# Selective scan in a vision stack: projection copies moved to the ends of units five and six, the copy of y behind the exps, the second projection behind the last spread

## The chip, the cores and the metric

The kernel runs on one core of a Trainium2 chip. The metric is device time in microseconds for one execution, given as the median of several. The engines are named as the profile names them: PE (TensorE matmuls), PEld (its weight loads), DVE (VectorE), ACT (ScalarE), POOL (GpSimd) and SP (SyncE, which here issues nearly all DMAs).

## The reference, cut to what matters

Four layers work on an image batch of shape (8, 64, 64, 96). Each layer normalises over channel groups, computes a residual and adds it. Layers 0 and 2 are selective scans in four directions: over rows, over columns, and both backwards. Layer 1 is a chunked scan, layer 3 a spectral filter with an expansion to 384 channels. The changed code belongs to the selective scan, whose core is this recurrence over the 4096 positions, for each direction k, each of 192 channels d and 16 states n:

```python
def step(h, inp):
    ut, dt, bt, ct = inp
    dA = jnp.exp(dt[..., None] * A4)
    dBu = (dt * ut)[..., None] * bt[:, :, None, :]
    h = h * dA + dBu
    y = jnp.einsum('bkdn,bkn->bkd', h, ct)
    return (h, y)
```

Here `dt` is a softplus of a projection of u, and `bt` and `ct` are two further projections of u. The sum of y over the four directions is kept.

## The kernel before, in words

The batch is a Python loop over eight images. For each image `selective_scan` is called twice (layers 0 and 2), so there are 16 passes. From the second image on, the last layer of the image before is laid in small operations (the class `Beside`) among the steps of the scan: 14 of the 16 passes have such work beside them.

A pass has 32 steps, one for each chunk: four directions k times eight chunks of 512 positions. In directions 1 and 3 the chunk is read along the columns of the image, so that its access to u and y is strided (`wh` is true). A chunk is made of six units: 32 channels times 16 states each, as 128 partitions times four groups of 512 positions. The loop `for t in range(total + 2)` goes over the units; n is the unit within the chunk (0 to 5), i the chunk. "The fifth and sixth unit" of the title are n = 4 and n = 5.

The order on every engine is the order in which the code emits the instructions (`tc.manual_schedule()`); an engine's queue works strictly in that order and waits by semaphores. Nothing is reordered by a planner.

What one unit needs:

- `spread` (L834): a matmul that lays 32 channels of delta times u over 128 partitions, into the PSUM tile pu. It shares a single buffer, tag "misc", with some operations of `Beside`.
- `with_b` (L840): the product of that with b, into db. Two units of three do it on DVE from pu, the third on POOL from a copy du2.
- `decays` (L855): two exps on ACT for each half of a unit, into the PSUM tile da of that half. There are only two such tiles, so the exps of a half can't begin before the scan of the same half of the unit before has ended.
- `scan` (L870): the recurrence on DVE, in two halves (p = 0 and 1); each half waits for its da and for db.
- `leave` (L886, L891): ACT copies the last state, POOL multiplies h by c in place.
- `total_y` (L898, L908): after three units PE sums over the states into the PSUM tile py; ACT then copies it to y (L993 for the first three units, L1007 for the others).

The PSUM tile py has the tag "py" and a single buffer. The same buffer serves the two projections pv of a coming chunk and some operations of `Beside`.

`prepare(i)` makes a chunk's inputs in parts, as a generator that is advanced by `prepare_part`. The parts, each ending at a `yield`, are: (1) the first projection, L742, into pv; (2) its copy into raw, L747, and the second projection, L751; (3) the copy of that, L755, its store to DRAM (bcd, L757) and the four loads of b (L764); (4) softplus, L775, and the stores of dd; (5) the loads of dx for the first three units (L782) and of c; (6) delta times u on POOL (L793, L799), its store and the loads of du2; (7) the loads of dx for the last three units (L782). SP issues these DMAs in the order of the code and stops at each until what it waits for has happened.

In the step of chunk i, part 1 of chunk i + 2 is emitted at the beginning of unit 4, part 2 in the middle of unit 5 (between the exps of its first and second half), part 3 in the middle of unit 0 of the next step, after `total_y` has been emitted; parts 4 and 5 at the ends of units 0 and 1, part 6 in unit 3, part 7 at the end of unit 5.

## Time and profile before

| | |
|---|---|
| median of three runs | 27086.93 us (27085.17 to 27111.33) |
| the profiled execution's own time | 27082.74 us |
| its span | 27080.9 us |
| instructions | 283056 |
| DVE busy | 23966.2 us, 88% |
| PE busy | 22624.0 us, 84% |
| POOL busy | 21781.7 us, 80% |
| ACT busy | 16539.7 us, 61% |
| scan halves on DVE (L870) | 6144, 2282 ns each |
| DVE idle just before a scan half | 900.6 us in all |
| granted TensorE clock, mean | 0.773 of full |

Times come from one profiled execution. A row of a group of instructions reads: line, engine, operation, output and inputs, shapes, count, then busy microseconds and the mean of one in nanoseconds, then the idle time of that engine just before them and what ended it. A row of the table of waits reads: who waited, for whom, microseconds in total, how often, the longest. A row of the timeline reads: start in microseconds, duration, engine, line, operation and count; in brackets the engine's idle time before it and what ended that. A row of the table of stretches gives for each engine the busy microseconds, then the granted TensorE clock, the share of the DMA engines and GB/s. PE's busy time is modelled, since matmuls are pipelined: a busy PE is not one at its peak.

### The profile page before, as it was taken

To read this page: it belongs to the slowest core of one execution; us is meant where nothing else is said; L and a number is where in the kernel's file an instruction comes from. 1 tells how busy PE (TensorE), PEld (TensorE's weight loads), DVE (VectorE), ACT (ScalarE), POOL (GpSimd) and SP (SyncE) were. 2 spreads that over 40 slices of the span, in tenths; PEclk is the share of its full clock that TensorE was granted. 3 is DMA by queue.
4 is the path that set the end of the run, shared out by engine and by line. 5 is a ranking of instruction groups with operands and counts; after the bars stand their busy time and mean duration, and the time that the engine had idled before them with its cause. 6 is when DMAs were issued, how large, how long until landed. Compare 5 with 4: busy or idle time off the path is not lost. (4 is left out here: it accounts for less than half of the span.)

```text
span 27080.9 us, 283056 instructions
## 1 busy us (share of the span) xinstructions
PE 22624.0 (84%) x91061; PEld 8150.5 (30%) x91061; DVE 23966.2 (88%) x17105; ACT 16539.7 (61%) x29953; POOL 21781.7 (80%) x8360
## 2 busy tenths in 40 slices
PE   7787788888888888888888888888888888888888
PEld 2141122422224222242222422224222342223424
DVE  8989899798997989979898898988989889898896
ACT  5656566466665656556565565655656556565564
POOL 8949898498984979859797697976979769797694
PEclk7687777877778777787777877778777787778878
DMA  4415454154541545415453254532545325453252
GB/s 121 119 30 124 114 130 117 31 131 122 132 111 35 133 117 137 103 44 132 116 136 98 50 132 118 135 92 56 133 119 134 85 62 133 118 134 78 70 133 67
DMA packets 1681704, 2831.72 MB, mean 105 GB/s; under 512 B 434984, under 2 KB 478280, under 8 KB 1675616
## 3 DMA queue, kind: packets, MB, share of 16 engines
q1 hardware_dynamic: 1663584, 2807.32, 41.9%
q8 instruction: 730, 11.96, 0.2%
q10 hardware_dynamic: 16640, 6.29, 0.1%
q14 instruction: 750, 6.14, 0.1%
HBM read 2385.11 MB, written 427.49 MB: 104 GB/s over the span
## 5 line engine op out<-in xcount | busy, mean ns | idle before, releaser
L870 DVE TENSOR_TENSOR_SCAN h<-da,db 128x1026 f32<-128x1026 f32 x6144 | 13765.8, 2282 | 900.6 <-ACT da L855 479.2
L891 POOL TENSOR_TENSOR h<-h,c 128x2048 f32<-128x2048 f32 x3072 | 12769.4, 4174 | 726.0 <-ACT state L886 510.1
L908 PE MATMUL py<-h,cst 128*32 128x512 f32 x24576 | 5301.4, 795 | 69.9 <-POOL h L891 69.8
L855 ACT ACTIVATE da<-dx,a2s 128x512 f32<-128x512 f32 x6144 | 4236.4, 690 | 1508.7 <-DVE h L870 1366.6
L855 ACT ACTIVATE da<-dx,a0s 128x512 f32<-128x512 f32 x6144 | 4235.8, 690 | 1481.8 <-DVE h L870 1344.3
L840 POOL TENSOR_TENSOR db<-du,b 128x2048 f32<-128x2048 f32 x1024 | 4648.2, 4539 | 567.6 <-ACT db L826 567.6
L840 DVE TENSOR_TENSOR db<-pu,b 128x2048 f32<-128x2048 f32 x2048 | 4643.9, 2268 | 110.9 <-PE pu L834 100.6
L834 PE MATMUL pu<-du,cst 32*128 32x512 f32 x4096 | 3239.2, 881 | 1007.4 <-DVE db L840 799.9
L908 PEld LDWEIGHTS py<-h,cst 128*32 128x32 f32 x24576 | 1175.0, 142 | 4827.3 <-issue 4517.4
L751 PE MATMUL pv<-u,wk 96*128 96x512 f32 x2048 | 1816.9, 1030 | 688.4 <-ACT raw L747 685.8
L898 PE MATMUL py<-y,cst 96*96 96x512 f32 x1536 | 1517.0, 1084 | 397.9 <-ACT raw L755 395.4
L834 PEld LDWEIGHTS pu<-du,cst 32*128 32x128 f32 x4096 | 790.4, 239 | 3079.7 <-issue 1361.9
L742 PE MATMUL pv<-u,wk 96*96 96x512 f32 x2048 | 1452.4, 838 | 186.7 <-ACT y L993 142.6
L1285 ACT ACTIVATE sg<-sg 128x768 f32<-128x768 f32 x1024 | 819.6, 800 | 859.1 <-PE sg L1269 859.1
L993 ACT COPY y<-py 96x512 f32<-96x512 f32 x512 | 417.5, 815 | 1411.4 <-PE py L908 1411.4
L516 PE MATMUL ps<-s,w3as 96*128 96x512 f32 x1344 | 912.4, 767 | 327.7 <-ACT sf L523 188.1
L1239 POOL TENSOR_TENSOR ce<-ec,cr 112x512 f32<-112x512 f32 x256 | 530.8, 2074 | 719.1 <-ACT ec L1237 700.8
L1317 DVE TENSOR_TENSOR wt<-wt,cbm 128x768 f32<-128x768 f32 x1024 | 985.3, 997 | 136.6 <-ACT wt L1286 136.1
L886 ACT COPY state<-h 128x4 f32<-128x4 f32 x3072 | 597.5, 194 | 782.5 <-DVE h L870 776.8
L751 PEld LDWEIGHTS pv<-u,wk 96*128 96x128 f32 x2048 | 540.6, 291 | 1740.2 <-ACT raw L747 1212.5
L319 POOL TENSOR_SCALAR xn<-xs,sb 96x512 f32<-96x512 f32 x192 | 198.1, 1033 | 991.7 <-PE pz L324 495.6
L1216 POOL TENSOR_TENSOR rr<-lr,cc 128x768 f32<-128x768 f32 x256 | 376.6, 1471 | 754.1 <-ACT lr L1214 749.2
(241 smaller groups left out, 30790.9 us busy)
## 6 DMA issues: line engine op xcount, KB each, us to landing
dx<-dd SPq DMA_DIRECT2D x4096, 192.0 KB
b<-bcd SPq DMA_DIRECT2D x2048, 256.0 KB
c<-bcd SPq DMA_DIRECT2D x2048, 256.0 KB
du<-dud SPq DMA_DIRECT2D x2048, 128.0 KB
dd<-raw SPq DMA_DIRECT2D x1024, 192.0 KB
dud<-du SPq DMA_DIRECT2D x512, 128.0 KB
xd<-xs SPq DMA_DIRECT2D x256, 192.0 KB
cr<-bcd SPq DMA_DIRECT2D x1536, 32.0 KB
```

The source lines that it names most:

```text
L516: nc.tensor.matmul(ps, w3as[:, m * 128 : (m + 1) * 128], live["x2"], start=True, stop=True)
L742: nc.tensor.matmul(pv[:DM], weights[k][:, hi, 128:], uv[hi], start=(hi == 0), stop=(hi == 1))
L751: nc.tensor.matmul(pv, weights[k][:, hi, :128], uv[hi], start=(hi == 0), stop=(hi == 1))
L834: nc.tensor.matmul(pu, sel[rows, :], m["du"][rows, n // 3, :], start=True, stop=True)
L840: (nc.gpsimd if pool else nc.vector).tensor_mul(groups(m["db", n]), (m["du2"][:, n // 3, :] if pool else m["pu"]) .unsqueeze(1) .to_broadc ...
L855: nc.scalar.activation(dst[:, g, :LC], made[i]["dx"][n // 3][:, n % 3, :], AF.Exp, scale=av4[:, k, n, gs : gs + 1],)
L870: nc.vector.tensor_tensor_scan(made[i]["h", n][:, at][:, way], das[p][:, rev : 2 * SEG + rev][:, way], made[i]["db", n][:, at][:, way], 0. ...
L891: nc.gpsimd.tensor_mul(h, h, made[i]["c"])
L898: nc.tensor.matmul(py, skip[:, hf, :] if k == 0 else ident[:DM, :DM], view((u if k == 0 else y)[:, hf, :], wh, c * LC, LC), start=True, st ...
L908: nc.tensor.matmul(py[32 * q : 32 * q + 32, :], red, hs[q][:, g, :], start=False, stop=(g == NSG - 1),)
L1285: nc.scalar.activation(sg, sg, AF.Abs)
L1317: nc.vector.tensor_mul(it["wt"], it["wt"], m["cbm"][:, j : j + 1, :].to_broadcast([128, RK, Q]),)
```

## The change

`prepare` gets one more `yield`: the copy of the first projection (L747) and the second projection (L751) become parts of their own, so that there are eight parts. In the step of chunk i they are now emitted as follows, for chunk i + 2: the first projection at the beginning of unit 4, as before; its copy at the end of unit 4; the second projection at the beginning of unit 5, right after that unit's spread; its copy, the store of bcd and the loads of b at the end of unit 5, ahead of the last part of chunk i + 1 (the dx loads of its last three units). The part in the middle of unit 0 is gone. The copy of y (L993) moves from the beginning of unit 4 to behind the exps of unit 5's first half, which unit 4 emits. On PE, DVE and POOL the order of the instructions stays what it was; ACT and SP are reordered.

```diff
@@ prepare
                 raw = tp.tile([128, 2, LC], F32, name="raw")
                 nc.scalar.copy(raw[:DM, 1, :], pv[:DM])
+                yield
 
                 pv = pyp.tile([128, LC], F32, name="pv", tag="py")
@@ before the loop
-                for _ in range(5):
+                for _ in range(6):
                     prepare_part(0)
...
-                for _ in range(2):
+                for _ in range(4):
                     prepare_part(1)
@@ the loop over units
                     elif n == 4:
-                        nc.scalar.copy(*sums)
                         if quota > 3:
                             other.begin(pmp, "misc")
                         prepare_part(i + 2)
-                    if n == 5:
+                    elif n == 5:
+                        prepare_part(i + 2)
                         other.end()
                     if t < total:
                         scan(t, 0)
...
                     elif n == 4:
+                        nc.scalar.copy(*sums)
                         other.end()
-                    elif n == 0:
-                        prepare_part(i + 1)
-                    elif n == 5:
-                        prepare_part(i + 2)
                     if t < total:
                         scan(t, 1)
                         leave(t, n == 3)
...
                     if n in (1, 2):
                         other.end()
+                    if n in (4, 5):
+                        prepare_part(i + 2)
                     if n in (0, 1, 5):
                         prepare_part(i + 1)
```

## The prediction

> **What bounds the kernel now.** I read the page's busy shares first, then its costliest groups, then the table of waits, then the timeline of single steps.

> ```profile
> PE 22624.0 (84%) x91061; PEld 8150.5 (30%) x91061; DVE 23966.2 (88%) x17105; ACT 16539.7 (61%) x29953; POOL 21781.7 (80%) x8360
> ...
> L870 DVE TENSOR_TENSOR_SCAN h<-da,db 128x1026 f32<-128x1026 f32 x6144 | 13765.8, 2282 | 900.6 <-ACT da L855 479.2
> L891 POOL TENSOR_TENSOR h<-h,c 128x2048 f32<-128x2048 f32 x3072 | 12769.4, 4174 | 726.0 <-ACT state L886 510.1
> ```

> DVE leads. The 6144 scan halves make 512 steps (16 passes of 32 chunks), each of six units u0 to u5. Per step DVE has 13765.8/512 = 26.9 us of scans and 4643.9/512 = 9.1 us of spreads times b (L840), 36.0 in sum; POOL has (12769.4 + 4648.2 + 737.1 + 615.2)/512 = 36.7, some 0.2 less where its instructions overlap. From one first scan half to that of the next chunk a step lasts 37.5 to 37.7 us on average and never under 36.2. So about 1.3 us of a step are waits of DVE, and POOL is free for about 1 us: no reordering can bring more than about 1 us x 512, some 500 us. The waits sit where one scan follows another with no spread product between them: before u5 (mean 0.72 us in the two passes without the last layer's operations beside, 0.44 to 0.47 in the others) and before u2 (0.62; 0.49 to 0.54). The table of waits names their neighbours:

> ```profile
> ACT y L993 <- PE py L908: 1411.4, 477, 6.6
> PE pv L751 <- ACT raw L747: 685.8, 432, 3.3
> PE py L898 <- ACT raw L755: 551.1, 479, 3.6
> DVE h L870 <- ACT da L855: 479.2, 563, 7.8
> ```

> ACT stands at the copy of y until TensorE has summed py, with the exps of u5 behind it; TensorE stands at the second projection and at the next total of y until ACT copies raw. Two steps show it, first one whose chunk is read along the rows ("plain"), without work beside:

> ```profile
> 261.13 4.48 DVE L870 TENSOR_TENSOR_SCAN h<-da,db 128x1026 f32<-128x1026 f32 x2
> ...
> 264.30 0.58 ACT L993 COPY y<-py 96x512 f32<-96x512 f32 x1 [3.81 <-PE py L908]
> 264.78 1.41 ACT L855 ACTIVATE da<-dx,a0s 128x512 f32<-128x512 f32 x2
> ...
> 264.93 1.96 PE L742 MATMUL pv<-u,wk 96*96 96x512 f32 x4 [0.75 <-ACT y L993]
> ...
> 266.28 4.48 DVE L870 TENSOR_TENSOR_SCAN h<-da,db 128x1026 f32<-128x1026 f32 x2 [0.66 <-ACT da L855]
> ...
> 266.82 1.12 PE L834 MATMUL pu<-du,cst 32*128 32x512 f32 x2
> ...
> 270.67 2.27 DVE L840 TENSOR_TENSOR db<-pu,b 128x2048 f32<-128x2048 f32 x1
> ```

> Then one whose chunk is read along the columns ("transposed", every second run of eight chunks), with work beside:

> ```profile
> 4386.01 4.48 DVE L870 TENSOR_TENSOR_SCAN h<-da,db 128x1026 f32<-128x1026 f32 x2
> ...
> 4388.39 1.05 ACT L993 COPY y<-py 96x512 f32<-96x512 f32 x1 [3.02 <-PE py L908]
> ...
> 4389.49 3.65 PE L742 MATMUL pv<-u,wk 96*96 96x512 f32 x4 [0.17 <-ACT y L993]
> ...
> 4393.08 2.07 PE L834 MATMUL pu<-du,cst 32*128 32x512 f32 x2
> ...
> 4395.18 2.29 DVE L840 TENSOR_TENSOR db<-pu,b 128x2048 f32<-128x2048 f32 x1
> ```

> Let z be the end of u4's first scan half (263.4; 4388.3) and W the start of the product with the next chunk's first spread (270.67; 4395.18). A second chain runs beside the scans: py ready, copy of y (one PSUM buffer, py, serves both), first projection, spread, product at W. In the plain step the spread was ready at 267.94, 2.7 us early. In the transposed step it ended at 4395.15 and the product began 0.03 later: there TensorE sets W already.

> **The change part by part.** [...]Durations are of this one execution, 27,082.7 us by its own time (span 27,080.9), 4.2 below the median of 27,086.9.

> 1. Copy of y behind u5's exps. The exps need z, end at z+1.47 and release scan u5 at once: W can then be z+6.5 (lowest value seen 6.47). But the copy cannot begin before z+1.47. Over 464 inner steps py ended at z-0.3 on average, and in 429 before z+1.36: in those y now waits for the exps and the first projection starts later than it could. The new chain is fixed: z+1.47, copy 0.58 (plain) or 1.05 (transposed), 0.06 to start, projection 1.96 or 3.65, spread 1.12 fast or 2.07 slow.
>    - Plain: 2.11 + 1.96 + 1.12 = z+5.2, below 6.5, so W = z+6.5. W before: z+7.21 without work beside (29 steps, scaled from 464 to 512), 7.03 with (131). Gain 0.71 x 29 + 0.53 x 131 = 90 us.
>    - Transposed: 2.58 + 3.65 - 0.1 (overlap) + about 1.9 = z+8.1. W before: 7.45 (26 steps), 7.08 (131). Loss 0.65 x 26 + 1.02 x 131 = 151 us. The cover of the late copy, the early start of this projection, is what is taken away.
>    - Plain copy with a transposed projection (chunks six and seven of a plain run): 2.11 + 3.65 + 1.6 = z+7.3 against 7.30 (9) and 6.63 (46): loss 31.
>    - Steps in which a second operation of the last layer comes ahead of that spread (139): its matmuls, its copy and the spread add about 3.2 us after the first projection where that is transposed. z+6.9 against 6.83 (70), 9.2 against 8.94 (15), 9.4 against 8.93 (54): loss 5 + 4 + 25 = 34.
>    - Sum +126 us. Where py is late, u4's remaining ACT work (side copy, state, exps' second half) now ends later than scan u5's second half wants: about +10.

> 2. Projection copies at the ends of u4 and u5 (fifth and sixth). The first copy waits for the first projection; queued behind it on ACT are the next chunk's first exps, the state of u5 and, after that, POOL's last product with c. The exps end at most 0.62 + 1.42 after the projection; the scan that wants them comes after a spread (1.1 at least) and a product (2.27): covered by construction. POOL takes up that last product at z+8.3 (263.37 + 8.29); the state is there at about z+8.5 in the worst, transposed case: nothing, at most 0.3 us of POOL's 1 us of slack. The second copy waits for the second projection (3.78 from the spread's end) and ends 4.4 after it; the exps behind it are wanted 2.27 + 2.24 = 4.5 after it: nothing.

> 3. Second projection behind the spread with no wait for ACT: the next total of y starts 1.0 us earlier (its idle before: 1.0 to 1.24 per step). The wait before u2 falls to 0.34, which stays, since there the exps follow the softplus with its two table loads. Gain 0.28 x 64 + 0.15 x 224 + 0.20 x 224 = 96 us.

> 4. SP. The store of bcd and the four b loads now stand ahead of the four dx loads for units u3 to u5, which before were issued at about z+4.3. In a transposed step: copy done z+12.6, b issued z+14.3 to 16.1, dx to z+17.9. The stretch 1018.5 to 1024 moved 199 GB/s at a DMA share of 0.81, some 240 GB/s when full, so b (1.05 MB), dx (0.79) and dd (0.39) are through by about z+24.3. u3's exps want dx at z+24.4 and delay a scan only after z+27.4, since a product precedes it. Cost 0; bounds 0 to +1 us per step. du, c and the first dx load have over 10 us of slack.

> 5. Before each pass one more copy and b's load: 16 x 0.6 at most, beside the convolution. Nothing.

> [...] TensorE's clock comes in whole stretches:

> ```profile
> 262.90:269.70 6.80, 4.29 (x15) 0.98 (x9) 6.14 (x4) 4.42 (x9) 6.80 (x3) 1.00 0.46 129
> 269.70:283.40 13.70, 11.83 (x23) 3.02 (x26) 13.49 (x7) 10.06 (x18) 13.70 (x4) 0.50 0.42 99
> ```

> (The column before the DMA share is the granted clock.) In the row the full clock outlives py's end (264.18) by 5.5 us. [...]

> Sum: 126 + 10 + 30 - 96 = +70: 27,082.7 + 70 = 27,153, say **27,150 us**, 0.23% above the median. 0.2% (54 us) is about what a measurement of this kernel can tell from no change.

> **Rivals.**
> - As worked out, chance 0.40: 27,040 to 27,260, since the transposed spread is uncertain by half a microsecond over 157 steps and the rest by as much again. 0.22 of it slower, 0.16 within the bound, 0.02 faster.
> - Faster, 0.30: the clock holds through the transposed projection, the spread takes 1.1 and W is z+7.2 instead of 8.1. 157 x 0.9 + 55 x 0.4 = 163 us less: 26,990; with plain steps keeping the clock on into the second projection and the total of y, 26,900. It decides where the full clock lasts beyond z+7.2. For: TensorE now runs on from the projection to the total of y without a pause. Against: in the transposed step the clock fell at 4393.0 with TensorE busy throughout. 0.05 of it stays within the bound.
> [...]
> - Slower by the dx loads, 0.05: they land after z+27.4 and the scan of u3 waits, 0.5 us x 512: 27,410. Against: 3 us of room by the sum above.

> Together: faster 0.02 + 0.25 = 0.27; within 0.16 + 0.05 = 0.21; slower 0.22 + 0.25 + 0.05 = 0.52. Below 26,880 and above 27,430 I leave about 0.1 each. Range 26,880 to 27,430.

> **What would show it.** Right: no wait of DVE before u5; the wait before u2 at 0.34; a wait of the product L840 on PE's pu grown from 100.6 us to 200 or more, in transposed steps; the row "PE pv <- ACT y" grown from 142.6 us, "PE pv <- ACT raw" and "PE py <- ACT raw" nearly gone. Plain steps near 36.5 us, transposed ones about 38. Wrong: transposed steps no longer than before, a wait of da on dx at u3, or a mean clock off 0.77 by over 0.02.

## The result, and the profile after

The changed kernel takes 27,477.0 us (median of four runs, 27,470.5 to 27,493.0); the kernel before took 27,091.6 in the four runs beside it. The ratio is 1.0142, with an interval of 1.0124 to 1.0159. It is 385 us slower; 70 had been predicted. The profiled executions lie 396 us apart by their spans (27,476.7 and 27,080.9), and the mean granted clock is 0.763 after 0.773. The sixteen passes take 409 us more from their first scan to their last, by the trace, so the whole loss is in them.

All comparisons below use the same lines of the code; in the changed kernel those from L751 on stand one line lower, and the moved copy of y is L1016. First the page's costliest groups, after:

```profile
L871 DVE TENSOR_TENSOR_SCAN h<-da,db 128x1026 f32<-128x1026 f32 x6144 | 13775.7, 2282 | 751.3 <-ACT da L856 446.0
...
L841 DVE TENSOR_TENSOR db<-pu,b 128x2048 f32<-128x2048 f32 x2048 | 4652.1, 2272 | 625.5 <-PE pu L835 616.7
...
L536 PE MATMUL ps<-w3bs,sf 128*128 128x96 f32 x5376 | 1043.9, 349 | 0.0
```

Then two rows of the table of waits, before and after:

```profile
PE pv L742 <- ACT y L993: 142.6, 215, 2.8
...
DVE db L840 <- PE pu L834: 100.6, 88, 3.3
```

```profile
DVE db L841 <- PE pu L835: 616.7, 388, 5.5
...
PE pv L742 <- ACT y L1016: 444.4, 295, 5.1
```

The scans themselves cost what they did, 2282 ns each. DVE's waits before scans went down, from 900.6 to 751.3 us; the waits before a spread product on PE's pu went up, from 100.6 to 616.7. The last layer's matmuls ran slower: L536 took 295 ns each before and takes 349 now, L516 767 and 833.

The trace splits the passes in two kinds. The two without work beside them got faster, from 1195.2 and 1194.9 us to 1185.0 and 1184.6. The fourteen with the last layer beside them went from 1197 to 1207 us up to 1223 to 1241. Mean steps, worked out from the scans' starts: without side work 37.32 to 36.60 us (plain) and 37.63 to 37.71 (transposed); with it 37.29 to 37.89 and 38.01 to 39.49.

One transposed step with side work shows the new end of the chain in the timeline (z is 7166.6):

```profile
7168.05 1.04 ACT L1016 COPY y<-py 96x512 f32<-96x512 f32 x1
...
7169.13 3.65 PE L742 MATMUL pv<-u,wk 96*96 96x512 f32 x4 [1.31 <-ACT y L1016]
...
7172.96 1.49 PE L536 MATMUL ps<-w3bs,sf 128*128 128x96 f32 x6
...
7176.65 2.04 PE L835 MATMUL pu<-du,cst 32*128 32x512 f32 x2 [0.50 <-ACT sg L547]
...
7178.73 2.29 DVE L841 TENSOR_TENSOR db<-pu,b 128x2048 f32<-128x2048 f32 x1 [5.36 <-PE pu L835]
```

The copy waits for the exps, the projection for the copy, a second operation of the last layer (the "fifth operation" below) runs behind the projection, and only then comes the spread. W is z+12.1, and DVE has stood for 5.36 us. The table of stretches for the same step, from z to the projection's end and from there to W (the column before the DMA share is the granted clock):

```profile
7166.60:7172.80 6.20, 4.89 (x11) 1.40 (x9) 6.15 (x4) 4.29 (x8) 6.20 (x3) 0.89 0.45 120
7172.80:7178.70 5.90, 5.40 (x19) 3.69 (x18) 0.57 (x1) 3.03 (x8) 3.54 (x2) 0.50 0.06 14
```

Everything behind the projection ran at half clock. In the trace's record of the clock the full one ends at 7171.44, so inside the projection, 2.3 us after TensorE had stood idle for 1.31 us.

### The profile page after: what moved, and what is told of

The parts are those of the page before. It is cut to its first block, busy times and chain, and to the rows that moved or that the text cites. A ratio compares the mean times of both kernels' runs of the same rounds, so it can differ in the third digit from the quotient of the medians.

```text
span 27476.7 us, 283336 instructions
## 1 busy us (share of the span) xinstructions
PE 23020.0 (84%) x91061; PEld 8527.1 (31%) x91061; DVE 24006.6 (87%) x17105; ACT 16531.6 (60%) x29953; POOL 21792.7 (79%) x8360
## 5 line engine op out<-in xcount | busy, mean ns | idle before, releaser
L871 DVE TENSOR_TENSOR_SCAN h<-da,db 128x1026 f32<-128x1026 f32 x6144 | 13775.7, 2282 | 751.3 <-ACT da L856 446.0
L892 POOL TENSOR_TENSOR h<-h,c 128x2048 f32<-128x2048 f32 x3072 | 12774.4, 4174 | 1129.8 <-ACT state L887 571.0
L841 DVE TENSOR_TENSOR db<-pu,b 128x2048 f32<-128x2048 f32 x2048 | 4652.1, 2272 | 625.5 <-PE pu L835 616.7
L835 PE MATMUL pu<-du,cst 32*128 32x512 f32 x4096 | 3328.7, 904 | 1203.6 <-DVE db L841 1070.1
L742 PE MATMUL pv<-u,wk 96*96 96x512 f32 x2048 | 1502.1, 864 | 556.6 <-ACT y L1016 444.4
L752 PE MATMUL pv<-u,wk 96*128 96x512 f32 x2048 | 1590.7, 911 | 54.3 <-ACT raw L747 53.3
L516 PE MATMUL ps<-s,w3as 96*128 96x512 f32 x1344 | 998.0, 833 | 544.8 <-ACT sf L523 188.1
L536 PE MATMUL ps<-w3bs,sf 128*128 128x96 f32 x5376 | 1043.9, 349 | 0.0
L536 PEld LDWEIGHTS ps<-w3bs,sf 128*128 128x128 f32 x5376 | 964.6, 263 | 0.0
```

The costliest lines, as they stand in the source:

```text
L516: nc.tensor.matmul(ps, w3as[:, m * 128 : (m + 1) * 128], live["x2"], start=True, stop=True)
L536: nc.tensor.matmul(po, live["f"][m][:, at : at + 128], w2q[:, m, :], start=False, stop=(m == 2),)
L742: nc.tensor.matmul(pv[:DM], weights[k][:, hi, 128:], uv[hi], start=(hi == 0), stop=(hi == 1))
L752: nc.tensor.matmul(pv, weights[k][:, hi, :128], uv[hi], start=(hi == 0), stop=(hi == 1))
L835: nc.tensor.matmul(pu, sel[rows, :], m["du"][rows, n // 3, :], start=True, stop=True)
L841: (nc.gpsimd if pool else nc.vector).tensor_mul(groups(m["db", n]), (m["du2"][:, n // 3, :] if pool else m["pu"]) .unsqueeze(1) .to_broadc ...
```

## Experiments

Two places were suspected. **A**: the copy of y held back behind the exps (step 1 of the prediction), with what follows it on TensorE. **B**: the rest of the change, that is the projection copies at the ends of units, the earlier total of y, the order of SP's loads. Lines of waits are quoted with each kernel's own line numbers; averages per step come from the traces. Times are medians; each ratio is to the kernel before on the same chip, and so are the distances in us. Where a kernel ran once there is no interval; the twelve runs of one kernel below, the one with both copies put back, spread over 68 us.

**The copy of y put back, all else as after**

```diff
                     elif n == 4:
+                        nc.scalar.copy(*sums)
                         if quota > 3:
...
                     elif n == 4:
-                        nc.scalar.copy(*sums)
                         other.end()
```

> The changed kernel with one part undone: the copy of y is again at the beginning of unit 4, ahead of unit 5's exps; the projection copies stay at the ends of units 4 and 5 and the second projection behind the last spread. Theory A (the held-back copy of y starts the first projection late, and that makes the spread product at W late): the loss goes and the gain before u2 stays, so about 27,087 - 96 = 26,990 us, in any case below 27,087; DVE's wait on pu falls from 617 us to about 110. Rival B (the copies at the unit ends block ACT, so that the exps come late): stays within 50 us of 27,477.

This is the kernel that later expectations call the one with y first. 27,349.8 us, ratio 1.0092 (1.0077 to 1.0107). Both expectations were missed: some 130 us came back, 250 stayed. So A alone doesn't explain the result. In the waits the place has changed:

```profile
DVE h L871 <- ACT da L856: 753.4, 724, 7.4
...
DVE db L841 <- PE pu L835: 178.0, 146, 3.3
```

The wait on pu is nearly gone, and the scans wait for their exps: before u5 by 1.02 and 1.08 us per step with side work, where in the kernel before it was 0.36 and 0.62 (plain, transposed).

**The copy of y alone moved, all else as before**

```diff
                     elif n == 4:
-                        nc.scalar.copy(*sums)
                         if quota > 3:
...
                     elif n == 4:
+                        nc.scalar.copy(*sums)
                         other.end()
```

> The kernel before with one part done alone: the copy of y behind the exps of unit 5, all projection copies where they were. Theory A: the whole loss and none of the gain before u2, so about 27,477 + 96 = 27,570 us. Rival B: 27,087 or less, since the wait of DVE before u5 (some 200 us) goes and nothing blocks ACT.

27,469.8 us, ratio 1.0136 (1.0121 to 1.0151): 371 us by this edit alone, 100 less than expected, and nearly all that the whole change costs.

```profile
PE pv L742 <- ACT y L1014: 697.3, 371, 5.1
...
DVE db L840 <- PE pu L834: 618.5, 357, 5.5
```

DVE's wait on pu is 618.5 us, as in the full change. The two parts, 371 and 250, make 621 one by one but 385 together: they hide behind each other.

**SP's order: the dx loads ahead of the store of bcd**

```diff
+                    if n in (0, 1, 5):
+                        prepare_part(i + 1)
                     if n in (4, 5):
                         prepare_part(i + 2)
-                    if n in (0, 1, 5):
-                        prepare_part(i + 1)
```

> The changed kernel with the DMA order of before on SP at that place: the dx loads of units 3 to 5 are issued ahead of bcd and the b loads at the end of unit 5. Theory A: no difference, 27,477 within 40 us. Rival C (the dx loads land late and hold the exps of u3): 27,100 to 27,400.

27,446.9 us, ratio 1.0126 (1.0111 to 1.0141). That is within the band expected if the order of DMAs doesn't matter, and its interval overlaps that of the changed kernel. The order of these loads explains at most some 40 of the 385 us, and not measurably that.

**The copy of y put back, and the second projection's copy too (middle of unit 0)**

```diff
# against the first experiment
-                for _ in range(4):
+                for _ in range(3):
                     prepare_part(1)
...
                     elif n == 4:
                         other.end()
+                    elif n == 0:
+                        prepare_part(i + 1)
...
-                    if n in (4, 5):
+                    if n == 4:
                         prepare_part(i + 2)
```

> Like the kernel with y first, but the second projection's copy, with bcd and b, is in the middle of unit 0 again, as before the change; the first copy stays at the end of unit 4 and the second projection starts right after the spread. If the gain before u2 comes from that second copy's place, it goes: the total of y waits for ACT again and the time is that of before, 27,087 within 50 us. If the earlier second projection alone brings it, the time is that of the kernel with y first, about 26,990.

27,103.1 us, ratio 1.0001 (0.9993 to 1.0010). The 250 us of the first experiment hang on the place of this one copy; the first copy at the end of unit 4 and the second projection behind the spread cost and bring nothing that can be measured. What the late copy does is visible in one row:

```profile
PE py L899 <- ACT raw L756: 900.7, 480, 3.2
```

TensorE waits again before the next total of y, 900.7 us in all (551.1 in the kernel before, where another 685.8 us were spent ahead of the second projection; here 177.6). This wait was step 3's to remove, and the kernel with it is the faster one.

**Why an earlier total costs time**

One plain step, the same in three kernels (the 18th of the fifth pass), TensorE's instructions just before u2's scan. Before:

```profile
7454.07 5.66 PE L908 MATMUL py<-h,cst 128*32 128x512 f32 x24
7459.66 1.12 PE L834 MATMUL pu<-du,cst 32*128 32x512 f32 x2
7460.71 0.46 PE L532 MATMUL ps<-w,s 96*128 96x96 f32 x2
7461.01 0.83 PE L536 MATMUL ps<-w3bs,sf 128*128 128x96 f32 x6
```

The first experiment's kernel, with the early total:

```profile
7461.91 4.24 PE L909 MATMUL py<-h,cst 128*32 128x512 f32 x20 [0.31 <-POOL h L892]
7466.09 1.12 PE L835 MATMUL pu<-du,cst 32*128 32x512 f32 x2
7469.74 0.51 PE L532 MATMUL ps<-w,s 96*128 96x96 f32 x2 [2.53 <-ACT y L1009]
7470.04 1.50 PE L536 MATMUL ps<-w3bs,sf 128*128 128x96 f32 x6
```

The total is done early, but ACT copies it to y at its old place in the queue (L1009 here, after exps that wait for a scan), and the last layer's operation waits for that copy: TensorE stands idle for 2.53 us. The next six L536 then take 1.50 us in place of 0.83. The table of stretches gives the 2 us ahead of u2's scan and the 6 us behind its start, before and then in the first experiment's kernel:

```profile
7457.85:7459.85 2.00, 2.00 (x13) 0.42 (x8) 1.21 (x1) 1.45 (x4) 1.49 (x1) 0.91 0.91 212
7459.85:7465.85 6.00, 5.18 (x35) 4.01 (x35) 6.00 (x3) 4.37 (x12) 4.27 (x2) 1.00 0.63 171
```

```profile
7467.26:7469.26 2.00, 0.00 (x0) 0.00 (x0) 1.66 (x2) 1.96 (x4) 2.00 (x1) 1.00 1.02 266
7469.26:7475.26 6.00, 5.11 (x24) 4.87 (x24) 6.00 (x3) 3.50 (x8) 5.40 (x2) 0.56 0.52 145
```

PE has 2.00 us of work in the first, none in the second, and the granted clock behind it is 1.00 and 0.56. At that clock the sum over the first three units is late, and u5 pays in the end (first experiment's kernel):

```profile
7488.86 0.58 ACT L994 COPY y<-py 96x512 f32<-96x512 f32 x1 [5.64 <-PE py L909]
...
7489.35 1.42 ACT L856 ACTIVATE da<-dx,a0s 128x512 f32<-128x512 f32 x2
...
7490.85 4.48 DVE L871 TENSOR_TENSOR_SCAN h<-da,db 128x1026 f32<-128x1026 f32 x2 [2.51 <-ACT da L856]
```

Over all plain steps with side work, PE is busy on average for 1.91 of those 2 us in the kernel before, for 0.54 in the first experiment's and for 0.78 in the changed kernel; the clock in the 6 us from the start of u2's scan is 0.88, 0.65 and 0.68.

If idleness is the cause, work without use in that place should bring the time back:

```diff
# against the first experiment
+    FILL = 2
...
                     elif n == 1 and t + 2 < total:
+                        if ops and 0 < i < len(steps):
+                            fill = pmp.tile([128, LC], F32, name="fill", tag="misc")
+                            for _ in range(FILL):
+                                nc.tensor.matmul(
+                                    fill, ident, made[i]["b"][:, 0, :], start=True, stop=True
+                                )
                         spread(t + 2)
```

> The kernel with y first, with two matmuls more per step (ident times b into a buffer nobody reads) in the 14 passes with work beside: on PE right behind the total of y, ahead of unit 3's spread, where PE now stands idle for about 2 us before unit 2. It only adds work. Theory D (the early total of y leaves PE idle there, the clock falls to half, the last layer's operations and py in units 2 and 3 run cold and the copy of y comes about 1 us later): granted clock up by 0.01 or more, the wait before u5 falls from 1.0 to 0.5 us and the time from 27,350 to 27,150 or less, at best 26,990. Rival E (something else than the clock makes py late, such as POOL or the order on ACT): 27,350 or more.

27,209.2 us, ratio 1.0050 (1.0033 to 1.0067). The kernel before took 27,072.5 beside it, so 137 us of loss are left of 250: about 115 came back by adding work. The clock and the plain steps moved as theory D has it, but the time stayed above its 27,150. The mean clock rose from 0.767 to 0.788, and the same step reads, first in the timeline of TensorE:

```profile
7455.55 1.98 PE L992 MATMUL fill<-b,cst 128*128 128x512 f32 x4
7457.59 1.12 PE L836 MATMUL pu<-du,cst 32*128 32x512 f32 x2
7459.44 0.46 PE L533 MATMUL ps<-w,s 96*128 96x96 f32 x2 [0.73 <-ACT y L1016]
7459.74 0.83 PE L537 MATMUL ps<-w3bs,sf 128*128 128x96 f32 x6
```

and in the table of stretches:

```profile
7456.97:7458.97 2.00, 1.69 (x4) 0.29 (x2) 1.66 (x2) 1.96 (x4) 2.00 (x1) 1.00 1.02 263
7458.97:7464.97 6.00, 4.71 (x34) 3.91 (x34) 6.00 (x3) 4.53 (x12) 5.97 (x3) 1.00 0.56 152
```

The wait is down to 0.73, the clock stays at 1.00, the six matmuls take 0.83 again and u5 doesn't wait. Plain steps went from 38.05 to 37.51 us on average, but transposed ones did not move (38.52 to 38.65). There the filler restores the clock too (0.80 to 0.92 in the 6 us from u2's scan on; 0.93 before), but pays for it in TensorE time. In 189 transposed steps the last layer's three operations between the copy of y and the next sum took 0.63 us less with it (6.36 after 6.99 us from the first matmul's start to the last one's end; 6.04 before), but the first began 0.79 us behind the copy instead of 0.05. So the sum is no earlier: it ends at z+0.20 after z+0.16. In 203 plain steps the three took 1.31 us less (6.11 after 7.42) and began 0.39 later.

**The same filler in the changed kernel**

> The changed kernel with the two filler matmuls behind the total of y, as in the y-first kernel with them. If the idle stretch before unit 2 is a separate part of the loss, the time falls by 96 us or more, to the held-back copy's own loss less the gain before u2: about 27,099 + 371 - 96 = 27,374 or less. If the held-back copy hides it (y waits for the exps anyway), it stays at 27,440 to 27,480.

27,482.4 us, ratio 1.0152 (1.0135 to 1.0169), though its mean clock is 0.781. Nothing comes back: DVE's wait on pu is 688.7 us. The sum ends earlier, at z+0.18 on average instead of z+0.58, but W in the 119 inner transposed steps with side work and no fifth operation stays at z+8.37 (8.36). With y held until the exps, a sum that is ready earlier isn't used; so the two parts overlap.

**No work beside at all** (the last layer is left out; three kernels: before, after, and the first experiment's)

```diff
-        pool, ops = slow_layer(prev) if prev else ([None], ((), ()))
+        pool, ops = [None], ((), ())
```

> The kernel before without the last layer's operations beside the scans: the last layer is computed for the last image alone, the others are left out. Every pass should last 1195 us as the first two do, so about 27,087 - 95 = 26,990 us.

> The changed kernel without the last layer's operations beside the scans (left out for all images but the last). Theory A with D: the loss is made only together with that work, so each pass lasts 1185 us and this is faster than the kernel before without it, by about 16 x 10 = 160 us (0.6%). Rival B (copies at the unit ends block ACT in every step): slower than it.

> The kernel with y first, without the last layer's operations (left out for all images but the last). Steps of 36.5 (plain) and 37.3 us (transposed) as in its first two passes: about 300 us (1.1%) faster than the kernel before without them. If the early total of y cost by itself, it would not be faster.

One run each: 26,965.2, 26,815.5 and 26,693.9 us. Without side work the change is 150 us faster, and without the held-back copy 271. Both were foreseen (160 and 300). So without side work the change does about what it was costed at; the held-back copy costs 122 us even here (the wait on pu is 385.9 us in the changed kernel), and the early total costs only with side work.

**The side copy moved to the end of unit 4**

```diff
                         nc.scalar.copy(*sums)
-                        other.end()
...
-                    if n in (1, 2):
+                    if n in (1, 2, 4):
                         other.end()
```

> The changed kernel with one move more: the copy of the last layer's operation begun in unit 4 goes behind the exps of u5's second half, instead of standing with the copy of y between the two pairs of exps. If that queue on ACT makes the wait before u5's second half (0.35 us per step with work beside, before the change 0.02), the wait goes to below 0.1 and the plain steps with work beside fall by 0.3 us or more, in sum 50 to 150 us: 27,330 to 27,430. If it is only the late py, nothing changes: 27,450 to 27,490.

27,436.4 us, ratio 1.0138 (1.0122 to 1.0153). That lies between the two bands; against the kernel before on its chip it is 369 us, within noise of the change's 385. The wait before u5's second half fell from 0.35 us to 0.04 or less per step, and the wait at W rose from 0.57 to 0.89 (plain) and from 1.73 to 2.00 (transposed). One wait passed to the next along the same chain; W is set by TensorE.

**Four operations per step at most** (a third of the last layer's hidden channels is left out, so there is never a fifth; also the mix is shorter; three kernels)

```diff
-            for m in range(3):
+            for m in range(2):
...
-                        for m in range(3):
+                        for m in range(2):
...
-                                stop=(m == 2),
+                                stop=(m == 1),
```

> The kernel before with a third of the last layer's hidden channels left out, so that no step has more than four of its operations and none stands ahead of unit 0's spread in unit 5. From the steps with and without a fifth operation: 27,090 - 120 = 26,970 us.

> The changed kernel with the same third left out. If the fifth operation, run behind the late projection, carries part of the loss as the classes of steps say (11.0 us after z in transposed steps with it, 8.4 without), this gains 230 us: 27,245, and its distance to the kernel before with the same cut is 275 us instead of 385. If that operation has no part in it, the distance stays 385 within 40.

> The y-first kernel with the same third of the hidden channels left out as in the pair before, so at most four operations per step. If the early total of y costs only through a fifth operation or a PE that is full, this is faster than the kernel before with the same cut (26,933), by up to 200 us. If the idle stretch costs in every step with work beside, it is 26,933 to 27,100.

One run each: 26,932.9, 26,955.7 and 26,897.7 us. The distance between before and after is 23 us, not the 275 expected, and the first experiment's kernel is 35 faster than before; neither is clear of the noise of single runs. So almost the whole loss needs the full side work. The edit takes away the fifth operation and also shortens others; the traces say at least in which steps the loss goes. In W - z, the measure used in the next section, all steps together lose 190 us between these two kernels and 459 between the full ones. The steps that have a fifth operation in the full kernels lose 41 instead of 213, the other steps with side work 148 instead of 245. So nearly two thirds of what goes lies in the steps that had the fifth operation.

**Projections read along the rows in every step** (the transposed read is left out, so the projections are of other positions)

```diff
-                uv = [view(u[:, hf, :], wh, at, LC) for hf in range(2)]
+                uv = [view(u[:, hf, :], False, at, LC) for hf in range(2)]
```

> The kernel before with both projections of every chunk read along the rows, also where the chunk is a transposed one: the inputs of those scans are thereby other than the reference's, the work is the same but for the stride. Transposed steps lose 1.7 us of PE time: 26,950 to 27,050.

> The changed kernel with the same edit. If the strided projection makes the held-back copy dear, transposed steps come near plain ones and the distance to the kernel before with the same edit is about 225 us or less, instead of 385. If the stride has no part, the distance stays 385 within 40.

One run each: 26,969.8 and 27,150.7 us. The distance is 181 us in place of 385, and DVE's wait on pu 243.5 us in place of 616.7. The stride of the projection carries about half of the loss. The kernel before gains by the edit itself, some 100 us on the 27,070.0 beside it, as expected.

**A version by pass**: the last kernel that stood level, and the second copy early only in the two passes without side work

```diff
# against the kernel with both copies put back
-                for _ in range(3):
+                for _ in range(3 if ops else 4):
                     prepare_part(1)
...
-                    elif n == 0:
+                    elif n == 0 and ops:
...
-                    if n == 4:
+                    if n == 4 or (n == 5 and not ops):
```

> The two orders put together: in the two passes without work beside, the order of the kernel with y first (second projection's copy at the end of unit 5); in the 14 passes with work beside, that copy in the middle of unit 0 as before the change. By the passes of these runs it should gain 2 x 18 us on the kernel before: about 27,060, a ratio of 0.9987. If it is within noise, 27,100.

27,065.8 us (eleven runs), ratio 0.9999 (0.9990 to 1.0008), so within noise. The two passes fell from 1195 to 1178 us each, the other fourteen rose by 10 in sum. No version here is measurably faster than the kernel before.

## Why the prediction was wrong in its size, point by point

The forecast was slower as the likeliest case, and the mechanism it named for that, the transposed projection behind the held-back copy, is there. The size was not: 70 us predicted, 385 measured, and the range ended at 27,430.

Two steps failed, and the run with the copy of y alone moved sizes them. Step 1, with its term for the clock, was put at 126 + 10 + 30 = 166 us; that run lost 371, so 205 are missing there. About two thirds of it lie in the steps with a fifth operation: in the prediction's own measure, W - z, their term was 34 and is 237 in that run, where all terms together were 126 and are 432. Step 3 was put at a gain of 96 us on top; on top of the moved copy the rest of the change is worth 385 - 371 = 14 us of loss, within noise, so 110 are missing there. Together this is the 315 us between 70 and 385.

The table gives W - z by kinds of steps for the whole change: means in us, inner steps only (29 of the 32 of a pass), and the terms in us over all 512 steps:

| steps | count, scaled | before | predicted | after | term predicted | term measured |
|---|---|---|---|---|---|---|
| plain, no side work | 29 | 7.21 | 6.5 | 6.48 | -21 | -21 |
| transposed, no side work | 26 | 7.45 | 8.1 | 8.15 | +17 | +18 |
| plain, then transposed projection, no side work | 9 | 7.30 | 7.3 | 7.70 | 0 | +4 |
| plain | 131 | 7.03 | 6.5 | 7.23 | -69 | +26 |
| plain, then transposed projection | 46 | 6.63 | 7.3 | 7.73 | +31 | +51 |
| transposed | 131 | 7.08 | 8.1 | 8.36 | +134 | +168 |
| plain, fifth operation | 70 | 6.83 | 6.9 | 7.89 | +5 | +74 |
| plain, then transposed projection, fifth | 15 | 8.94 | 9.2 | 10.74 | +4 | +27 |
| transposed, fifth | 54 | 8.93 | 9.4 | 10.99 | +25 | +111 |

The measured terms sum to about +458, the predicted ones to +126. W - z is one stretch of a step; waits elsewhere in it fell, so the time grew by less.

- **Step 1, the fixed chain: right without side work.** There the projection began at z+2.09 (plain) and z+2.47 (transposed), predicted 2.11 and 2.58, and W came within 0.1 us in both; for a plain copy with a transposed projection it was 0.4 late. The runs without side work agree with it in sum (150 us gained, about 175 by its terms).
- **Step 1, "py ended at z-0.3 on average": a premise that fell, but not what cost most.** It was read from the trace of before and taken over to after. After, py ends at z+0.58 on average, and only 292 of 464 inner steps (429 before) have it by z+1.36. With side work the projection starts at z+2.4 to 3.0, by class, not 2.1 to 2.6, and the 69 us gain of plain steps became a loss of 26. But in the run with the copy of y alone moved py ends at z-0.22, about as assumed, and 371 us are lost all the same.
- **The fifth operation, "about 3.2 us": undersized, and the largest miss.** In transposed steps the time from the projection's end to the spread's end was 3.44 us before, 4.53 after and 4.78 with the copy of y alone moved; the mean granted clock in it was 0.93, 0.71 and 0.64. With the projection late by the held-back copy, this operation's matmuls run in part at half clock, as in the step shown. +34 predicted, +212 measured.
- **"Late second half of u5, +10":** that wait grew by 0.33 us a step, which is 148 us over 448 steps, but moving the copy that causes it gave no time back. It is not a term of its own.
- **Step 2, the copies cost "nothing": right for ACT's queue, wrong for what they release.** The exps were covered as worked out. But the second copy's early place is what makes the total early, and this is worth 250 us of loss by itself.
- **Step 3, the gain of 96 us: failed as a net gain; the wait went, and other waits took its place.** The wait before u2 is 0.34 us per step in all four classes, some 92 us less than before. What was not asked is what TensorE does with the time it gains: it waits for the copy of y that ACT makes at its old place. Alone this costs 250 us; beside the held-back copy it adds nothing that can be measured.
- **Step 4, SP, and step 5, the prologue: right.** Loads of dx in either order give the same time within the intervals, and what lies outside the passes' scans moved by 13 us in all (396 against 409).
- **The clock: looked for in the wrong place.** Between z+2 and z+4 plain steps with side work kept a mean clock of 0.95, as before, so no run shows the 30 us that stand in the sum for the clock; even the 83 of them before whose py ended ahead of z-1.3 kept 0.88. (With the copy of y alone moved, and the sum early, it is 0.85 there.) The clock fell around u2, where the change opens idle time that the trace of before could not show (0.68 after 0.88 in the 6 us from u2's scan on, plain steps with side work), and behind the projection (0.50 in the step shown). In the step of the first experiment's kernel it was 0.56 in the 6 us from u2's scan on, with an idle stretch of 2.53 us around that start, and 1.00 with the filler, where the idle stretch was 0.73.
- **The rivals.** Faster fell: W in transposed steps is z+8.36, not 7.2. Of the chances for slower, the 0.25 stood for a clock that falls before z+4. That is the right agent for a part of the loss in the wrong place: from z+2 to z+4 plain steps with side work stayed at 0.95. Slower by dx (27,410) came nearest in time, with the wrong cause: with those loads first again the kernel stayed at 1.0126.
- **"What would show it"** named rows that came true in direction: no wait before u5's first half (0.08), 0.34 before u2, the wait on pu grown to 616.7, "PE pv <- ACT y" from 142.6 to 444.4, "PE pv <- ACT raw" down from 685.8 to 53.3. The step lengths (36.5, 38) hold for passes without side work alone, and the clock's move, 0.010, stayed under the 0.02 given as a warning: a mean hid what a 6 us stretch shows as 1.00 and 0.56.

What the runs show in sum: the copy held back costs 371 us alone and the early total 250 alone; together 385. About half of the 385 goes when the projection is not strided, and nearly all of it when the side work is smaller: 150 us are gained without any, 23 lost with a third of its hidden channels left out. The filler shows that idle time before u2 is a cause of the early total's loss. That the clock behind the projection makes the fifth operation dear is read from the traces; no run took that clock alone away.

## What to carry to other kernels

Where a wait of one engine is removed, ask which instruction it reaches next and whether that waits for something whose place has not moved; here the total came earlier, its copy did not, and the wait turned into idle time. A dated quantity from the trace of before ("py ends at z-0.3") can be carried over only if nothing upstream of it moves, the clock included: look for stretches in which the change leaves TensorE without work, all around the loop. Passes or steps of the same loop with and without side work should be summed apart, as they can answer with opposite signs.
